# More places for y late in the first pass, weight matrices laid over the passing adjacency tiles, and the powers and copies of x reordered at the seam

## The chip, the cores and the metric

The kernel runs on one core of one Trainium2 chip. The metric is the device time of one execution in microseconds, as a median over several runs. A profile was taken of one more execution; its span and the times inside it are given separately from the median.

## What is computed

Inputs are node features `x` (4096 x 512), an adjacency matrix `adj` (4096 x 4096, fp32) and weights. The matrix has the diagonal and about two entries in a thousand beside it, all below one. Two layers follow each other:

```python
# layer 0
a = adj + eye
d = sum(a, axis=1) ** -0.5
out = relu((d[:, None] * a * d[None, :]) @ x @ W.T + b)
x = layernorm(x + out)
# layer 1: 8 heads
adj1 = maximum(adj, eye)
scores = q @ k.T / sqrt(64) + 0.01 * eye - 1e16 * (1 - adj1)
x = layernorm(x + sum over heads of softmax(scores) @ v @ Wo)
```

All entries beside the diagonal are below one, so the term with 1e16 leaves only the diagonal in the softmax. Layer 1 is then a product of each row with one fixed matrix. The kernel uses this, and tests for it at the end; a general version would run if the test failed.

## The kernel before

All that matters here is in `few_edges_below_one` (L420 to L1328). The 4096 rows are cut into 32 tiles of 128. The work has two passes.

**First pass** (loop at L1004, t = 0 to 32). Each step takes one adjacency tile of 128 x 4096 (2 MB), loaded by SP three steps ahead (`load_first`, L559). Of the 32 tiles, 12 are *early* (0, 2, 4, 6, 9, ... 24) and 5 are *resident* (27 to 31). These lie in five buffers of the pool `big` under the name `a_t`, and stay until their entries are extracted. The other 15 only pass through, in two buffers named `a_n`, and are loaded again in the second pass. The last tile is loaded in two halves.

Per tile, ACT sums the rows (`sum_rows`, L691), or, for an early tile, only looks for negative entries (`sum_negative`, L696), since DVE gives the row sum of an early tile out of its extracted entries (L926). POOL makes the degree factor out of the sum (`scaling`: an addition at L703 and a power at L706, written to `d_all`). Beside this, x of each tile is loaded by POOL (`load_x`, L549), transposed by PE (L672), copied out of PSUM by ACT (`evacuate`, L677, to `xT`) and multiplied by the transposed weights on PE (`times`, L684, to a PSUM buffer `acc`; two buffers for xT, five for acc). ACT then multiplies the product by d (`keep_y`, L711, to `y_t`, four buffers), and POOL writes it to the DRAM tensor `y` (L713).

The list `due` (L984) says at which step each tile's y is made: a tile that is not early at t + 1, an early one later, when DVE has its sum. The xT copy and the product are issued one step ahead, two from step `EARLIER` = 25 on. A scheduler orders the instructions of each engine by priority and readiness. `keep_in_program_order` holds marked instructions of an engine in the order in which the program has them; the y copies are marked, the xT copies are not.

The second layer's matrix `wvo` is made in the same steps from Wv and Wo (`second_weights`). Wo and the transposed Wv lie in a buffer of the first pass named `wo` (16 KB per partition), which is last read by the products at L619.

DVE meanwhile extracts the entries of the tiles (`extraction`): per tile eight segments, each with a search for the eight largest (L740) and for their places (L741), then short steps that sort them into records. `some((t + 1) * RATE)` paces this: 7 of 16 steps per loop step, the rest in the second pass. `match` spreads the records over 128 lanes so that nine gathers per tile are enough.

**The seam** (L1049 to L1219). The pool of the first pass is closed, and two pools are opened in its memory: `second` (gathered rows `g`, own rows `yo`, `h`, and others) and then `mats` (three selection matrices `s_t` of 128 x 9 or 10 x 128, and `sq`). 18 gathers are issued ahead, and 14 selection matrices are built.

**Second pass** (loop at L1235). For each tile, POOL gathers nine times 128 rows of y from DRAM by index (L1066; 19 buffers). PE multiplies each by its selection matrix (L1269) and adds in PSUM. ACT builds the selection matrices (`spread`, L964 to L977). DVE scales, adds bias and residual (`scaled` L1135, `residual` L1143). The norm is folded into the last steps: PE transposes h (L672), ACT copies it (L677), PE multiplies by wvo (L684), ACT writes the result. DVE goes on with extraction up to the 28th of the 32 tiles.

Of the kernel before, what the change touches and what calls it, by code (L numbers as in the profile page):

```python
# [9 lines left out]
FP = mybir.dt.float32  # L10
# [4 lines left out]
P = 128  # L15
# [404 lines left out]
def few_edges_below_one(  # L420
# [18 lines left out]
    nc = tc.nc  # L439
    N, D = x.shape  # L440
# [31 lines left out]
    ps_t = ctx.enter_context(tc.tile_pool(name="ps_t", bufs=3, space=bass.MemoryType.PSUM))  # L472
    ps_a = ctx.enter_context(tc.tile_pool(name="ps_a", bufs=5, space=bass.MemoryType.PSUM))
    first = ExitStack()
    p1 = first.enter_context(tc.tile_pool(name="first", bufs=2))

    ident = const.tile([P, P], FP, name="ident")
# [62 lines left out]
    def load_a(t, pool=big, name="a_t", parts=1):  # L540
        a_t = pool.tile([P, N], FP, name=name)
        for c in range(parts):
            o = ts(c, N // parts)
            nc.sync.dma_start(a_t[:, o], adj[ts(t, P), o])
        return a_t
# [8 lines left out]
    early = [e * last // EARLY for e in range(EARLY)]  # L554
# [4 lines left out]
    def load_first(t, parts=1):  # L559
        if t in early or t in resident:  # L560
            return load_a(t, parts=2 if t == NT - 1 else parts)
        return load_a(t, p1, "a_n")

    a_tiles = {0: load_first(0, 4)}


# [6 lines left out]
    wT = p1.tile([P, ND, D], FP, name="wT", bufs=1)  # L573
# [10 lines left out]
    def load_second_weights():  # L584

        nc.sync.dma_start(
            wv.rearrange("p (h f) -> p h f", h=H),
            wvs.rearrange("h (p j) k -> p h (j k)", j=ND),
        )
        su1 = p1.tile([P, 2, ND, D], FP, name="wo", bufs=1)  # L590
        nc.sync.dma_start(su1[:, 0], wo.rearrange("(r a) k o -> (a k) r o", a=2))
        return su1

    def order_second_weights():
        nc.gpsimd.tensor_copy(
            w_nat.rearrange("p j (h k) -> p j h k", h=H),
            wv.rearrange("p (h j k) -> p j h k", h=H, j=ND),
        )
# [70 lines left out]
    def transpose_rows(src, dcs=range(ND)):  # L669
        pt = ps_t.tile([P, 512], FP, name="pt")  # L670
        for dc in dcs:
            nc.tensor.transpose(pt[:, ts(dc, P)], src[:, ts(dc, P)], ident)  # L672
        return pt

    def evacuate(pool, name, pt):
        dst = pool.tile([P, ND, P], FP, name=name, bufs=2)
        nc.scalar.copy(dst.rearrange("p c s -> p (c s)"), pt[:, :D])  # L677
        return dst

    def times(srcT, w, u=None, dcs=range(ND)):  # L680
        if u is None:
            u = ps_a.tile([P, D], FP, name="acc")
        for dc in dcs:
            nc.tensor.matmul(  # L684
                u, srcT[:, dc, :], w[:, dc, :], start=(dc == 0), stop=(dc == ND - 1)
            )
        return u

    def sum_rows(dst, part):
        dump = wk_.tile([P, N], mybir.dt.uint8, name="dump")  # L690
        nc.scalar.activation(dump[:, : part.shape[1]], part, AF.Copy, accum_out=dst)  # L691

    def sum_negative(t, a_t, halves=(0, 1)):
        dump = wk_.tile([P, N], mybir.dt.uint8, name="dump")
        o = slice(halves[0] * N // 2, (halves[-1] + 1) * N // 2)
        nc.scalar.activation(  # L696
            dump[:, o], a_t[:, o], AF.Relu, scale=-1.0,
            accum_out=neg_all[:, t, halves[0] : halves[0] + 1],
        )

    def scaling(t, more=None):
        deg = small.tile([P, 1], FP, name="deg")
        nc.gpsimd.tensor_scalar(deg, deg_all[:, t : t + 1], 1.0, None, op0=ALU.add)  # L703
        if more is not None:
            nc.gpsimd.tensor_tensor(deg, deg, more, ALU.add)
        nc.gpsimd.tensor_tensor(d_all[:, t : t + 1], deg, mhalf, ALU.pow)  # L706

    def keep_y(t, u):
        y_t = p1.tile([P, D], FP, name="y_t", bufs=4)
        tc.keep_in_program_order(  # L710
            nc.scalar.activation(y_t, u, AF.Copy, scale=d_all[:, t : t + 1])  # L711
        )
        nc.gpsimd.dma_start(y[ts(t, P), :], y_t)  # L713
# [164 lines left out]
    def match(*stages):  # L878
        for stage in stages:
            n = staged[stage]  # L880
            if stage == KEY:
                ready = n < len(sorted_)
            elif stage == PERM:
                ready = n < staged[RANKS] and n - staged[MOVE] < 2
            else:
                ready = n < staged[stage - 1]
            if stage == ACROSS:
                ready = ready and n == staged[RANKS]
            if stage == MOVE:
                ready = ready and n == staged[END]  # L890
            if not ready:
                continue
            t = order[n]
            e = edges[t]
            if stage == KEY:
                e["key"] = match_key(t)
            elif stage == ACROSS:
                e["pk"] = match_across(e["key"])
            elif stage == RANKS:
                e["rank"] = match_ranks(e["key"], e["pk"])  # L900
            elif stage == PERM:
                e["perm"] = match_perm(e["rank"])
            elif stage == MOVE:
                e["pm"] = match_move(e["rec"], e["perm"])
            else:
                match_end(t, e["pm"])
                matched.add(t)
            staged[stage] += 1
# [34 lines left out]
    def some(upto):  # L943
        while count[0] < upto:
            count[0] += 1
            next(work, None)
# [33 lines left out]
    xs, us = {}, {}  # L980
    DEEP = 3
    RATE = 7
    EARLIER = NT - 7
    due = [(t + 1, t) for t in range(NT) if t not in early]  # L984
    for n, t in enumerate(early):
        at = max(t + 3, -(-STEPS * (n + 1) // RATE) + 1)
        taken = [j for j, _ in due]
        due.append((next((j for j in (at, at + 1) if j not in taken), at), t))
    due.sort()
    fetch = [t for _, t in due]  # L990

    def prefetch(count):
        for _ in range(count):
            if fetch:
                t = fetch.pop(0)
                xs[t] = load_x(t, nc.gpsimd, p1, 6)

    prefetch(5)
    for t in range(1, DEEP):
        a_tiles[t] = load_first(t)  # L1000
# [3 lines left out]
    for t in range(NT + 1):  # L1004
        if t == 0:
            su1 = load_second_weights()
        if t + DEEP < NT:
            a_tiles[t + DEEP] = load_first(t + DEEP)
        if t == 3:
            order_second_weights()  # L1010
            setup = second_weights(su1)

        lo, hi = t + 1 + (t > EARLIER), t + 1 + (t >= EARLIER)
        ahead = [j for at, j in due if lo <= at <= hi]
        pts = []
        for j in ahead:
            prefetch(1)
            pts.append(transpose_rows(xs.pop(j)))
        kind, begin, end = next(setup, (None,) * 3) if len(ahead) < 2 else (None,) * 3
        got = begin() if kind == "t" else None  # L1020
        if t < NT:
            if t in early:
                sum_negative(t, a_tiles[t])
            else:
                sum_rows(deg_all[:, t : t + 1], a_tiles[t][:, : N // 2 if t == NT - 1 else N])
                more = None
                if t == NT - 1:
                    more = small.tile([P, 1], FP, name="more")
                    sum_rows(more, a_tiles[t][:, N // 2 :])
                scaling(t, more)  # L1030
            if t in again:
                del a_tiles[t]
        if left:
            left()
            left = None
        for j in [j for at, j in due if at == t]:
            if j in early:
                scaling(j)
            keep_y(j, us.pop(j))
        for j, pt in zip(ahead, pts):  # L1040
            us[j] = times(evacuate(p1, "xT", pt), wT)
        if kind == "t":
            end(got)
        if kind == "p":
            left = lambda end=end, pa=begin(): end(pa)
        if t < NT - 5:
            match(*ALL)
        some((t + 1) * RATE)
# [2 lines left out]
    second.append(True)  # L1051


    p2 = ctx.enter_context(tc.tile_pool(name="second", bufs=2))
    mat = ctx.enter_context(tc.tile_pool(name="mats", bufs=3))
    AHEAD = 18

    SUMMED = (NT - 2, NT - 1)
# [151 lines left out]
    yo, zs, hs, pts, hTs, ws, sts, mats, halves = ({} for _ in range(9))  # L1210
# [24 lines left out]
    for i in range(NT + 2):  # L1235
# [3 lines left out]
        p = i - 1  # L1239
        has_p = 0 <= p < NT  # L1240
        for k in range(KH):
            ends = p == NT - 1
            t = at("T", i, k)
            if t not in (None, NT - 1):
                hTs[t] = evacuate(p2, "hT", transpose_rows(hs[t]))
            t = at("M", i, k)
# [50 lines left out]
            t = at("Q", i, k)  # L1297
# [3 lines left out]
            t = at("V", i, k)  # L1301
# [6 lines left out]
            t = at("F", i, k)  # L1308
# [45 lines left out]
```

## Time and profile before

| | us |
| --- | --- |
| median of 3 runs | 652.62 (651.55 to 655.58) |
| profiled execution | 689.3 |
| its span on the core | 687.5 |
| PE busy in the span | 555.8 |
| DVE busy | 546.9 |
| ACT busy | 509.7 |
| POOL busy | 352.0 |
| last load of adjacency in the first pass has landed | 213.4 |
| last y copy ends | 226.7 |
| first gather is issued | 230.1 |
| first product of the second pass starts | 236.6 |

Times inside the span count from its start. A row of the timeline gives start, duration, engine, line, operation, output from input with shapes, the number of instructions merged, and in square brackets the time for which the engine stood idle before it and what ended that wait. Matmuls in fp32 show as two records each, so a product of a 128 x 512 tile with the 512 x 512 weights has eight. Busy shares are means over stages with different limits; which wait ends last has to be read stage by stage. The end of a matmul is modelled.

### The profile page before, as it was taken

What the parts mean: (1) busy time and instruction counts of PE and PEld (TensorE: products, weight loads), DVE (VectorE), ACT (ScalarE), POOL (GpSimd) and SP (SyncE); (2) the same over time, 40 slices, a digit from 0 to 9 for tenths busy, and PEclk for the clock granted to TensorE, in tenths of its full rate; (3) what the DMA queues carried; (4) which work ended last, traced back from release to release, by engine and by line L of the source; (5) the groups of instructions that cost most, each with busy time, mean ns of one, the idle gap of its engine ahead of it and who ended that gap; (6) DMA issues with size and microseconds to landing.
All of it is one profiled execution on the core that took longest, in us unless ns stands there. A gap on an engine that the chain in (4) does not pass through costs nothing. (4 is left out here: it accounts for less than half of the span.)

```text
span 687.5 us, 7941 instructions
## 1 busy us (share of the span) xinstructions
PE 555.8 (81%) x1604; PEld 257.1 (37%) x1604; DVE 546.9 (80%) x2141; ACT 509.7 (74%) x1121; POOL 352.0 (51%) x464
## 2 busy tenths in 40 slices
PE   1688795897884284779978999889897989899994
PEld 1343342343441132334433444334343434344442
DVE  6679999999999725689978999799999888442441
ACT  1778859778759833799876888779897779789642
POOL 4222322412323575667666566666676676557620
PEclk9999898999997597999998999999999999999998
DMA  8999999999992677999999799999998977868731
GB/s 338 401 418 427 421 428 408 419 422 418 421 423 114 227 207 250 391 328 370 409 401 344 233 369 358 335 325 346 345 366 311 351 239 234 260 215 263 231 105 51
DMA packets 51850, 222.14 MB, mean 323 GB/s; under 512 B 8080, under 2 KB 9104, under 8 KB 45520
## 3 DMA queue, kind: packets, MB, share of 16 engines
q1 hardware_dynamic: 18416, 119.55, 43.3%
q0 software_dynamic: 28240, 92.56, 39.5%
q10 hardware_dynamic: 5136, 9.44, 3.6%
q14 instruction: 43, 0.35, 0.1%
q8 instruction: 15, 0.25, 0.1%
HBM read 204.73 MB, written 16.78 MB: 322 GB/s over the span
## 5 line engine op out<-in xcount | busy, mean ns | idle before, releaser
L1066 POOL DMA_INDIRECT g<-y,cols_all x288 | 282.1, 980 | 148.3 <-issue 67.4
L1269 PE MATMUL acc<-g,s_t 128*128 128x512 f32 x540 | 256.7, 615 | 23.0 <-ACT s_t L977 22.4
L740 DVE MAX8 v_all<-a_t 128x8 f32<-128x512 f32 x256 | 170.7, 679 | 17.9 <-DMA a_t<-in_adj_dram 17.4
L741 DVE FIND_INDEX8 idx<-v_all,a_t 128x8 uint32<-128x512 f32 x256 | 174.3, 683 | 0.0
L1269 PEld LDWEIGHTS acc<-g,s_t 128*128 128x128 f32 x540 | 101.5, 197 | 135.8 <-issue 109.8
L684 PE MATMUL acc<-wT,xT 128*128 128x512 f32 x256 | 123.6, 634 | 27.0 <-ACT xT L677 24.8
L684 PE MATMUL acc<-wvo,hT 128*128 128x512 f32 x256 | 118.2, 604 | 12.4 <-issue 6.0
L696 ACT ACTIVATE dump<-a_t 128x2048 uint8<-128x2048 f32 (+1 forms) x52 | 119.4, 2296 | 1.5 <-DMA a_t<-in_adj_dram 1.5
L684 PEld LDWEIGHTS acc<-wT,xT 128*128 128x128 f32 x256 | 49.9, 203 | 88.1 <-issue 54.2
L684 PEld LDWEIGHTS acc<-wvo,hT 128*128 128x128 f32 x256 | 48.1, 192 | 76.8 <-issue 64.0
L964 ACT ACTIVATE sq<-cols,wr_all 128x128 f32<-128x128 f32 x160 | 57.7, 392 | 2.4 <-DMA y<-y_t 2.4
L968 ACT ACTIVATE s_t<-sq,wr_all 128x128 f32<-128x128 f32 x128 | 57.1, 483 | 0.5
L691 ACT ACTIVATE dump<-a_n 128x4096 uint8<-128x4096 f32 x15 | 54.3, 3622 | 0.6 <-DMA a_n<-in_adj_dram 0.3
L549 POOL DMA_DIRECT2D x_t<-in_x_dram x32 | 17.9, 560 | 63.0 <-PE pt L672 62.8
L977 ACT ACTIVATE s_t<-s_t,wr_all 128x128 f32<-128x128 f32 x150 | 48.5, 390 | 0.6 <-ACT s_t L974 0.6
L753 DVE MAX8 top<-key 128x8 f32<-128x64 f32 x192 | 39.9, 215 | 5.6 <-DVE h L1135 1.3
L1135 DVE SCALAR_TENSOR_TENSOR h<-acc,d_all,yo 128x512 f32<-128x512 f32 (+1 forms) x33 | 23.8, 721 | 21.0 <-remote 18.4
L711 ACT ACTIVATE y_t<-acc,d_all 128x512 f32<-128x512 f32 x32 | 21.5, 684 | 21.0 <-POOL d_all L706 16.3
L713 POOL DMA_DIRECT2D y<-y_t x32 | 19.0, 592 | 29.6 <-ACT y_t L711 28.7
L703 POOL TENSOR_SCALAR deg<-deg_all 128x1 f32<-128x1 f32 x32 | 6.9, 230 | 48.3 <-ACT dump L691 48.2
L1170 ACT ACTIVATE sums<-sums 128x1 f32<-128x1 f32 x32 | 6.3, 197 | 33.8 <-DVE sums L1165 10.3
L1128 DVE SCALAR_TENSOR_TENSOR yo<-yo,own_all,b_bc 128x512 f32<-128x512 f32 x32 | 23.7, 741 | 9.4 <-issue 8.7
(126 smaller groups left out, 652.7 us busy)
## 6 DMA issues: line engine op xcount, KB each, us to landing
a_t<-in_adj_dram SPq DMA_DIRECT2D x30, 2048.0 KB
a_n<-in_adj_dram SPq DMA_DIRECT2D x15, 2048.0 KB
x_t<-in_x_dram POOLq DMA_DIRECT2D x32, 256.0 KB
y<-y_t POOLq DMA_DIRECT2D x32, 256.0 KB
yo<-y SPq DMA_DIRECT2D x32, 256.0 KB
x_t<-in_x_dram SPq DMA_DIRECT2D x32, 256.0 KB
out_dram<-r_t ACTq DMA_DIRECT2D x32, 256.0 KB
g<-y,cols_all POOLq DMA_INDIRECT x288
```

The lines of the kernel that those rows point to most:

```text
L684: nc.tensor.matmul(u, srcT[:, dc, :], w[:, dc, :], start=(dc == 0), stop=(dc == ND - 1))
L691: nc.scalar.activation(dump[:, : part.shape[1]], part, AF.Copy, accum_out=dst)
L696: nc.scalar.activation(dump[:, o], a_t[:, o], AF.Relu, scale=-1.0, accum_out=neg_all[:, t, halves[0] : halves[0] + 1],)
L740: long.append(lambda o=o, seg=seg: nc.vector.max(v[:, o], seg))
L741: long.append(lambda o=o, seg=seg: nc.vector.max_index(idx[:, o], v[:, o], seg))
L753: return lambda: nc.vector.max(top[:, f, r * 8 : r * 8 + 8], keyf[:, f])
L964: nc.scalar.activation(sq, cols1, AF.Square, bias=wr[:, 2, k : k + 1])
L968: nc.scalar.activation(s_t[:, k, :], away(), AF.Relu, scale=wr[:, 3, k : k + 1], bias=wr[:, 1, k : k + 1],)
L977: nc.scalar.activation(s_t[:, k, :], s_t[:, KH, :], AF.Copy, scale=wr[:, 1, k : k + 1])
L1066: nc.gpsimd.indirect_dma_start(out=slots[j], out_offset=None, in_=y[:, :], in_offset=bass.IndirectOffsetOnAxis(ap=cols_all[:, t, k : k + 1 ...
L1135: nc.vector.scalar_tensor_tensor(hs[i][:, c], zs[i][:, c], d_all[:, order[i] : order[i] + 1], yo[i][:, c], op0=ALU.mult, op1=ALU.add,)
L1269: nc.tensor.matmul(zs[i], mats[i][:, k, :], slots.pop(i * KH + k), start=(k == 0), stop=(k == KH - 1),)
```

## The change

Four things are altered; no instruction is removed or added, only order, memory and waits differ.

1. The passing adjacency tiles `a_n` get a pool of their own, `passing`, opened ahead of the pool `first`. At the seam `mats` is opened ahead of `second`, so that the matrices lie where the passing tiles were.
2. The y of tiles that are due at step 20 or later (15 of the 32) goes to one of eight places in a buffer that takes over the memory of `wo`. The others keep the four buffers.
3. The degree factor of an early tile is asked for before the step's row sum and not just before its y copy.
4. The xT copies issued from step 25 on are marked to stay in program order among the marked instructions of ACT.

```diff
     first = ExitStack()
+    pn = first.enter_context(tc.tile_pool(name="passing", bufs=2))
     p1 = first.enter_context(tc.tile_pool(name="first", bufs=2))
...
-        return load_a(t, p1, "a_n")
+        return load_a(t, pn, "a_n")
...
-    def evacuate(pool, name, pt):
+    def evacuate(pool, name, pt, pinned=False):
         dst = pool.tile([P, ND, P], FP, name=name, bufs=2)
-        nc.scalar.copy(dst.rearrange("p c s -> p (c s)"), pt[:, :D])
+        copy = nc.scalar.copy(dst.rearrange("p c s -> p (c s)"), pt[:, :D])
+        if pinned:
+            tc.keep_in_program_order(copy)
         return dst
...
     def keep_y(t, u):
-        y_t = p1.tile([P, D], FP, name="y_t", bufs=4)
+        if t in due_first:
+            y_t = p1.tile([P, D], FP, name="y_t", bufs=4)
+        else:
+            if not y_bank:
+                y_bank.append(p1.tile([P, 8, D], FP, name="wo", bufs=1))
+            y_t = y_bank[0][:, y_count[0] % 8]
+            y_count[0] += 1
         tc.keep_in_program_order(
             nc.scalar.activation(y_t, u, AF.Copy, scale=d_all[:, t : t + 1])
         )
...
     due.sort()
+    due_first = [t for j, t in due if j < 20]
+    y_bank, y_count = [], [0]
     fetch = [t for _, t in due]
...
         got = begin() if kind == "t" else None
+        for j in [j for at, j in due if at == t and j in early]:
+            scaling(j)
         if t < NT:
...
         for j in [j for at, j in due if at == t]:
-            if j in early:
-                scaling(j)
             keep_y(j, us.pop(j))
         for j, pt in zip(ahead, pts):
-            us[j] = times(evacuate(p1, "xT", pt), wT)
+            us[j] = times(evacuate(p1, "xT", pt, t >= EARLIER), wT)
...
+    mat = ctx.enter_context(tc.tile_pool(name="mats", bufs=3))
     p2 = ctx.enter_context(tc.tile_pool(name="second", bufs=2))
-    mat = ctx.enter_context(tc.tile_pool(name="mats", bufs=3))
```

## What was predicted

> **What bounds the kernel now.** I read the page first (busy times, the forty slices, the costliest groups), then busy time by stage, then ACT's timeline from 140 to 230 us, then the timelines around the seam between the passes. The chain of waits at the end of the page covers only the last microsecond and says nothing on the seam.
>
> ```profile
> PE 555.8 (81%) x1604; PEld 257.1 (37%) x1604; DVE 546.9 (80%) x2141; ACT 509.7 (74%) x1121; POOL 352.0 (51%) x464
> ...
> PE   1688795897884284779978999889897989899994
> PEld 1343342343441132334433444334343434344442
> DVE  6679999999999725689978999799999888442441
> ACT  1778859778759833799876888779897779789642
> ```
>
> No engine is full overall, but each stage has its own limit. The first pass runs against DMA (its slices are 9 up to about 206 us), with DVE full from about 100 us. The second pass has PE at nine tenths and DVE nearly so. Between them, near slices 12 to 15, everything thins out. By stage (columns: stretch, length, PE, PEld, DVE, ACT, POOL busy, granted clock, DMA share, GB/s):
>
> ```profile
> 200.00:210.00 10.00, 8.23 (x15) 3.55 (x16) 10.00 (x30) 6.07 (x7) 1.61 (x4) 0.83 0.82 345
> 210.00:220.00 10.00, 4.20 (x10) 1.44 (x8) 10.00 (x42) 8.42 (x6) 3.65 (x8) 0.84 0.22 86
> 220.00:230.00 10.00, 0.00 (x0) 0.00 (x0) 10.00 (x45) 7.13 (x13) 3.52 (x8) 0.50 0.20 79
> 230.00:240.00 10.00, 3.42 (x4) 1.47 (x5) 5.99 (x20) 10.00 (x31) 7.70 (x8) 0.50 0.95 320
> ```
>
> From 214 to 236 us PE does nothing and DMA is nearly empty: no gather may start until every row of y is in DRAM, and ACT is late with the last rows. ACT's timeline says why:
>
> ```profile
> 198.87 0.59 ACT L677 COPY xT<-pt 128x512 f32<-128x512 f32 x1 [3.06 <-PE pt L672]
> 201.03 0.69 ACT L711 ACTIVATE y_t<-acc,d_all 128x512 f32<-128x512 f32 x1 [1.57 <-DMA y<-y_t]
> 204.62 0.69 ACT L711 ACTIVATE y_t<-acc,d_all 128x512 f32<-128x512 f32 x1 [2.90 <-DMA y<-y_t]
> ...
> 205.67 3.63 ACT L691 ACTIVATE dump<-a_t 128x4096 uint8<-128x4096 f32 x1
> ...
> 215.64 1.26 ACT L711 ACTIVATE y_t<-acc,d_all 128x512 f32<-128x512 f32 x2 [1.58 <-POOL d_all L706]
> ...
> 226.01 0.69 ACT L711 ACTIVATE y_t<-acc,d_all 128x512 f32<-128x512 f32 x1 [0.44 <-POOL d_all L706]
> ...
> 229.37 0.69 ACT L964 ACTIVATE sq<-cols,wr_all 128x128 f32<-128x128 f32 x2 [2.40 <-DMA y<-y_t]
> ```
>
> By the completions in the trace the last six loads of adjacency landed at 188.2, 194.2, 200.2, 206.1, 209.7 and 213.4 us. Their sums began at 192.1, 205.7, 210.3, 216.8, 221.0 and 223.0: ACT is 4 us behind its data at tile 27 and over 10 us behind at tiles 28 to 30. In between it stood for 3.06 + 1.57 + 2.90 + 1.58 + 0.44 = 9.6 us. From the last y the seam goes on like this:
>
> ```profile
> 230.13 1.06 POOL L1066 DMA_INDIRECT g<-y,cols_all  x1 [2.59 <-DMA y<-y_t]
> ...
> 236.58 5.72 PE L1269 MATMUL acc<-g,s_t 128*128 128x512 f32 x8 [22.39 <-ACT s_t L977]
> ```
>
> The PE wait is put down to ACT, but that s_t was done before 232.2; the first gather's increments arrive until 235.8, and that is the later one.
>
> **What the Trainium skill says.** "TensorE: Matmul & The Clock Gate", Architectural detail: ScalarE's queue is strictly first in, first out. The trace agrees: the sum of tile 28, whose data landed at 194.2, stands behind two y copies until 205.7. The same page, Part 1: PE's clock is half or full, and about 3.4 us of sustained work lift it. Agrees: from 236.58 the matmul records follow each other at 0.85 us until 240.1, then at 0.43. "DMA: Bandwidth & Descriptors", Anatomy of one DMA: about 2 us of a transfer are fixed, mostly the receipt. Agrees: last y issued 227.00, its readers free at 229.3 to 229.4.
>
> **The change, part by part.** *Eight places for y (tiles due at step 20 or later, 15 of the 32).* A y copy reuses a place after eight others and not four. It takes away the two waits on y's DMA, 1.57 + 2.90 = 4.5 us of ACT; no instruction is added. What is late next behind them is the xT copy and the sum of tile 28.
>
> *d_all asked for ahead of the row sum.* POOL's 0.2 us addition and 0.57 us power of an early tile now stand before the step's x load and y write in POOL's queue, not behind. Before 230 us ACT waits 16.3 us in 12 places for d_all; some 1.7 and 1.8 us of these lie shortly before tile 27 (at 162 and 175 us), 1.58 at 214. I count 2 us ahead of 192 and the 1.58. POOL issues the same DMAs; it is 16 to 36% busy there, so the order costs it nothing. Without that cover a 0.8 us pair per step would delay an x load.
>
> *xT copies pinned from step 25.* This one costs. The built order of ACT now has, from the sum of tile 27: sum, y y, xT xT, sum, y, xT, sum, y y, xT xT, sum, y, half, half, xT, y, y. Before, all xT copies were through by 210.4 and the last product by 214.2, so the last y waited only 0.44 us. Now tile 31's xT stands after both halves of the last sum, its product and its y follow in series.
>
> *Matrices laid over the passing tiles.* The sq copies no longer share memory with y's places, so ACT does not wait 2.40 us at 227. Nothing is gained on the path: PE's first product waits for the gather. The cover is those 6 us from issue to landing. If the gather landed at once, it would be worth up to 2.4. The order of PE, SP and POOL after the seam is the same in both programs.
>
> The sum, on the profiled time scale. ACT from tile 27's sum to the end of the last half: 4 sums at 3.7 (start to next start), 2 halves at 2.05, six y at 0.58, five xT at 0.47: 14.8 + 4.1 + 3.5 + 2.4 = 24.8 us. Starting at 190 (192.1 less the 2) with 1 us for a product that is not ready: 215.8. The floor from the data is 213.4 + 2.1 = 215.5. I take 216. Then xT 0.6, eight matmul records 3.5 at 0.43 or 6.9 at 0.85 (PE idles some 2 us before, so partly slow; I take 4.5), y 0.7: 221.8, against 226.7. With the early ends (190, fast clock) it is 220.4, with the late ones (192.1, slow clock) 226.3: a gain of 0.4 to 6.3, taken as 4.9. From the last y to the first gather nothing changes (3.4 us), so gathers start near 225.2 and PE near 231.7.
>
> What of it arrives at the end? DVE is full until 235 and then idles 6.5 us waiting for PE's product at 242.5, so it gives 4.9 us without becoming the bound at once. In the 50 us stretches from 300 to 600 us PE is busy 41 to 47, DVE 37 to 48: PE leads, but waits for DVE some 17 us over them (6.5 of it for permutations, the rest for keys and records). So I keep three quarters: 3.7 us. The lower bound is 0 (DVE's work sets the pace to 575 us), the upper the whole.
>
> The profiled execution took 689.3 us (span 687.5), the timed median is 652.62, 36 less. About half of that shows as one stall:
>
> ```profile
> 265.33 0.75 DVE L1135 SCALAR_TENSOR_TENSOR h<-acc,d_all,yo 128x512 f32<-128x512 f32 x1 [18.43 <-remote]
> ```
>
> It needs only PE's first accumulation, recorded as over at 246.8. I take it for a feature of this execution and carry the difference, not the level: 652.6 - 3.7 = 648.9, say 649.
>
> **The rivals.** *Swallowed.* DVE, full from 100 us on, sets the pace of the second pass and the 4.9 us turn into PE waits. For it: DVE idles only some 27 us from 270 to 550. Against: those 27 us and the 6.5 at the seam. Time 652.6, within 2.
>
> *PE's clock makes the new series long: slower.* From the first xT after tile 27's sum (about 195) PE has six products one after another, each behind an xT that ACT now gives late. At full clock they need 6 x 3.44 = 20.6 us and end at 216, hidden. All slow they need 41 and end at 236; the last y is then at 237, 10 us later than now: 663. It decides where a product takes over (226.0 - 195) / 6 = 5.2 us, that is, where half of the 48 records run slow. For it: the clock was 0.83 between 200 and 220, and PE gets more pauses. Against: the 24 records from 201.77 lost only 12.43 - 10.3 = 2.1 us, those from 187.94 (10.46 us) none.
>
> *Larger.* The timed runs hold part of the 18.4 us stall and a seam with less crowding shortens it, or all 9.6 us of ACT's waits go and the second pass keeps them: 643, with the whole stall 630. For it: nothing but the stall's place. Against: the data floor at 213.4 us.
>
> **How the numbers follow.** Main case 0.50 at 649, its own range 646 to 651.5; swallowed 0.15; slower 0.18 (656 to 663, 0.15 of it above 1%); larger 0.17. About 1% (6.5 us) is what a measurement of this kernel can tell from no change. Faster by more: the larger case plus 0.05 from the main one's end, 0.22. Slower by more 0.15. Within 0.63. The range 641 to 658 leaves out half of the larger and half of the slower case.
>
> **What would show it.** Right: no wait on y's DMA ahead of ACT's y copies after 190 us, tile 28's sum starting before 200, the last y at 220 to 224, the first gather at 223 to 227, the 2.40 us at sq gone. Right on the cost: a PE wait of 3.5 to 7 us before the last y. Wrong: the last y at 226 or later, matmul records at 0.85 us through 200 to 225, or PE's second-pass waits for DVE grown by as much as the seam shrank. A changed time while the seam stands still would say that none of this is the cause.

## The result and the profile after

The changed kernel took 650.0 us (median of 16 runs, one of which took 1033.8 us), the kernel before 654.4 us on the same chip: a ratio of 0.9946, 95% interval 0.9924 to 0.9969. The medians differ by 4.4 us; the ratio, from which that one run is left out, says 3.5 us, with an interval from 2.0 to 5.0. The 3.7 us that were predicted lie inside it, and so do the 4.9 that the seam was to give. The likeliest case held. Its parts did not: two of the steps were wrong, and their errors cancelled.

The profile of before that the prediction used, and one set of experiments (e1 to e4, on another chip than the other sets; before: 686.8 us there, 653 to 654 in the others), belong to a level at which the same program takes some 33 us longer, so times are compared only within a set.

The page of the changed kernel (busy times, then busy tenths of a slice of 16 us):

```profile
PE 556.8 (86%) x1604; PEld 258.0 (40%) x1604; DVE 543.6 (84%) x2141; ACT 509.1 (79%) x1121; POOL 351.2 (54%) x464
...
PE   1698696888689486999999989999999999999794
...
DVE  5679999999999994999999979999999996532431
ACT  1868888779779775999898957999979989994433
```

At the seam PE has one slice of four tenths, where it had slices of 4, 2 and 4, and later it stays at nine tenths. Part of this belongs to the first profile of before and not to the change: e9, a later profile of the same kernel, has PE at nine tenths from 400 us on as well. The stages around the seam (stretch, length, PE, PEld, DVE, ACT, POOL busy, clock, DMA share, GB/s):

```profile
200.00:210.00 10.00, 9.94 (x32) 4.98 (x31) 10.00 (x33) 8.69 (x7) 2.13 (x5) 1.00 0.93 385
210.00:220.00 10.00, 7.21 (x17) 2.72 (x15) 10.00 (x43) 6.72 (x12) 3.21 (x7) 1.00 0.17 66
220.00:230.00 10.00, 1.33 (x2) 0.50 (x2) 10.00 (x44) 10.00 (x33) 5.77 (x7) 0.60 0.69 249
230.00:240.00 10.00, 9.78 (x26) 3.94 (x25) 10.00 (x38) 5.99 (x14) 7.59 (x8) 0.89 0.77 233
```

PE's products for the last tiles now run to 219 us at full clock (1.00 from 200 to 220), and the gathers begin inside the third stretch. ACT's timeline of the changed kernel over the same time:

```profile
187.18 3.62 ACT L694 ACTIVATE dump<-a_t 128x4096 uint8<-128x4096 f32 x1
...
192.75 0.69 ACT L720 ACTIVATE wo<-acc,d_all 128x512 f32<-128x512 f32 x1 [1.28 <-PE acc L687]
...
194.34 3.62 ACT L694 ACTIVATE dump<-a_t 128x4096 uint8<-128x4096 f32 x1
...
199.45 3.62 ACT L694 ACTIVATE dump<-a_t 128x4096 uint8<-128x4096 f32 x1 [0.21 <-DMA a_t<-in_adj_dram]
...
214.72 0.57 ACT L678 COPY xT<-pt 128x512 f32<-128x512 f32 x1
...
219.13 0.69 ACT L720 ACTIVATE wo<-acc,d_all 128x512 f32<-128x512 f32 x1 [3.25 <-issue]
```

The sums of tiles 27, 28 and 29 start at 187.2, 194.3 and 199.5, the last of them as soon as its load has landed. No y copy waits for y's DMA here. The last half sum ends at 214.7; in series with it follow the last xT, its product (3.70 us on PE) and the last y. The 3.25 us ahead of the last y are put down to issue, but PE's product ends only then. The gathers, from POOL's timeline:

```profile
223.25 1.06 POOL L1077 DMA_INDIRECT g<-y,cols_all  x1 [2.59 <-DMA y<-wo]
```

Against the recorded signs: tile 28 before 200, the first gather within 223 to 227 and no 2.40 us wait at sq, all as said; the last y ends at 219.8, just under the 220 to 224 that was given, and its wait is 3.25 us, just under 3.5 to 7. The wait on y's DMA after 190 us is gone as said, but this sign turned out to tell nothing: two later profiles of the kernel before (e1, e9) do not have it either.

### The profile page after: what moved, and what is told of

The parts are those of the page before. It is cut to its first block, busy times and chain, and to the rows that moved or that the text cites. A ratio compares the mean times of both kernels' runs of the same rounds, so it can differ in the third digit from the quotient of the medians.

```text
span 645.5 us, 7946 instructions
## 1 busy us (share of the span) xinstructions
PE 556.8 (86%) x1604; PEld 258.0 (40%) x1604; DVE 543.6 (84%) x2141; ACT 509.1 (79%) x1121; POOL 351.2 (54%) x464
## 5 line engine op out<-in xcount | busy, mean ns | idle before, releaser
L1280 PE MATMUL acc<-g,s_t 128*128 128x512 f32 x540 | 258.1, 612 | 23.8 <-DMA g<-y,cols_all 13.4
L749 DVE MAX8 v_all<-a_t 128x8 f32<-128x512 f32 x256 | 172.7, 687 | 16.9 <-DMA a_t<-in_adj_dram 16.9
L1280 PEld LDWEIGHTS acc<-g,s_t 128*128 128x128 f32 x540 | 98.0, 194 | 140.9 <-issue 92.8
L687 PE MATMUL acc<-wT,xT 128*128 128x512 f32 x256 | 126.6, 647 | 24.1 <-ACT xT L678 24.0
L687 PEld LDWEIGHTS acc<-wvo,hT 128*128 128x128 f32 x256 | 49.7, 196 | 67.4 <-issue 58.1
L1146 DVE SCALAR_TENSOR_TENSOR h<-acc,d_all,yo 128x512 f32<-128x512 f32 (+1 forms) x33 | 24.0, 727 | 20.9 <-PE acc L1280 15.9
L678 ACT COPY hT<-pt 128x512 f32<-128x512 f32 x31 | 17.9, 579 | 23.8 <-PE pt L673 22.8
L673 PE MATMUL pt<-ident,x_t 128*128 128x128 f32 x128 | 20.3, 291 | 8.8 <-DVE above L841 7.6
L765 DVE MATCH_REPLACE8 key<-top,key 128x64 f32<-128x64 f32 x128 | 27.2, 214 | 0.0
```

The costliest lines, as they stand in the source:

```text
L687: nc.tensor.matmul(u, srcT[:, dc, :], w[:, dc, :], start=(dc == 0), stop=(dc == ND - 1))
L749: long.append(lambda o=o, seg=seg: nc.vector.max(v[:, o], seg))
L765: return lambda: nc.vector.match_replace(keyf[:, f], top[:, f, r * 8 : r * 8 + 8], keyf[:, f], 0.0)
L1280: nc.tensor.matmul(zs[i], mats[i][:, k, :], slots.pop(i * KH + k), start=(k == 0), stop=(k == KH - 1),)
```

## The experiments

The theory after this result was: the seam moved by 6.9 us (226.7 to 219.8), 4.4 arrive, so the second pass gives some back, because gathers are delayed by the first reload of an adjacency tile. The rival was that DVE or PE sets the pace there and swallows it. The other question was which of the four parts moves the seam.

| kernel | first gather | span of that profile | gather to end | median less before's in its set |
| --- | --- | --- | --- | --- |
| before (e9) | 227.13 | 652.5 | 425.4 | -0.7 |
| changed | 223.25 | 645.5 | 422.3 | -4.4 |
| changed (e5) | 223.90 | 647.2 | 423.3 | -4.6 |
| no overlay (e6) | 224.61 | 650.5 | 425.9 | -2.7 |
| reload later (e7) | 225.19 | 653.8 | 428.6 | +1.2 |
| last xT first (e8) | 222.47 | 646.7 | 424.2 | -4.7 |
| no pin (e10) | 225.25 | 649.4 | 424.2 | -1.9 |
| seam later (e11) | 231.97 | 654.5 | 422.5 | +4.4 |
| early d_all alone (e12) | 232.61 | 659.0 | 426.4 | +4.7 |
| set with the longer time: before (e1) | 226.87 | 684.4 | 457.5 | +1.9 |
| no pin (e2) | 226.15 | 682.3 | 456.2 | -1.9 |
| no bank (e3) | 238.15 | 693.2 | 455.1 | +9.0 |
| no early d_all (e4) | 230.99 | 689.5 | 458.5 | +3.7 |

One reading needs the whole table. In the rows above the set with the longer time, e7 left aside since it alters the second pass, the first gather comes 3.9, 3.2, 2.5, 4.7 and 1.9 us earlier than e9's (changed, e5, e6, e8, e10) or 4.8 and 5.5 us later (e11, e12). The medians lie 4.4, 4.6, 2.7, 4.7 and 1.9 us below before's, or 4.4 and 4.7 above. The end moves with the first gather and by about as much; the two numbers differ by 1.3 us at most.

The first gather has a spread of its own. ACT's order in the first pass is the same in the changed kernel, e5, e6 and e7, and the first gather comes at 223.25, 223.90, 224.61 and 225.19. A difference of 1 to 2 us between two single profiles therefore shows little.

**The kernel before again (e1, e9).** No edit.

> The kernel before, unchanged, for a second profile of it. Ratio 1.00. Theory 1 (gathers give the gain back): the seam stands as in the first profile (last y at 225.5 to 228, PE's first second-pass product at 235 to 238, so 7 to 8 us later than in the changed kernel), but PE loses 3 to 4 us less than the changed kernel in the first five tiles of the second pass, because fewer of its gathers fall under the first reload of an adjacency tile. Theory 2 (DVE sets the pace): the first five tiles take as long as in the changed kernel (within 1 us), and the changed kernel loses the 3 to 4 us between 260 and 560 us to PE waits on DVE.

Ratio 1.0014 (0.9987 to 1.0040). It belongs to the set with the longer time, so its second pass says nothing about the changed kernel's. Its seam does, since the first pass takes the same time in both (last y at 222.8 here, 223.0 in e9).

> The kernel before, unchanged, for a profile at the level of its timed runs. Ratio 1.00. Theory (the seam's gain, less what the opening of the second pass loses): first gather 226.5 to 230.5 (223.3 and 223.9 in the two profiles of the changed kernel), the ninth h (the first tile after eight) 4 to 6 us later than the changed kernel's 343.1 and 343.8, the end later by the same, so what is lost of the seam is lost before 345 us. Rival (DVE or PE sets the pace later): ninth h 6 to 7 us later than in the changed kernel, the difference shrinking to 4 only after it.

Ratio 0.9987 (0.9964 to 1.0010). First gather at 227.13, ninth h at 347.9 against 343.1 and 343.8, and the end 5.3 to 7.0 us later than in the two profiles of the changed kernel. The difference does not shrink after the ninth h, so the rival falls, and it is no smaller at the end than at the first gather (3.2 to 3.9), so nothing is lost before it either. The 5.3 to 7.0 are too large, though: e9's profiled execution took 1.7 us more than its kernel's median, that of the first profile of the changed kernel 2.7 us less. ACT's timeline of e9:

```profile
200.47 0.59 ACT L677 COPY xT<-pt 128x512 f32<-128x512 f32 x1 [3.06 <-PE pt L672]
...
202.56 3.65 ACT L691 ACTIVATE dump<-a_t 128x4096 uint8<-128x4096 f32 x1
...
212.63 1.26 ACT L711 ACTIVATE y_t<-acc,d_all 128x512 f32<-128x512 f32 x2 [1.67 <-POOL d_all L706]
...
223.01 0.69 ACT L711 ACTIVATE y_t<-acc,d_all 128x512 f32<-128x512 f32 x1 [0.44 <-POOL d_all L706]
...
226.37 0.69 ACT L964 ACTIVATE sq<-cols,wr_all 128x128 f32<-128x128 f32 x2 [2.40 <-DMA y<-y_t]
```

Here is the first surprise. The two waits on y's DMA that the prediction took as its main term (1.57 and 2.90 us at 201 and 205) are in none of these two later profiles. The 2.40 us at sq and the wait of 3.06 us on PE are.

**Without the pin (e2, e10).**

```diff
-            us[j] = times(evacuate(p1, "xT", pt, t >= EARLIER), wT)
+            us[j] = times(evacuate(p1, "xT", pt), wT)
```

> The changed kernel without the pin on the xT copies. Theory 1 (the series xT, product, y after the last sum costs 4.4 us at the seam): last y ends at 215.5 to 217.5 and not 219.8, time 1 to 3 us less than the changed kernel (647 to 649). Rival (the pin is what keeps ACT's sums from standing behind an xT copy that waits for PE's transposes): waits of 2 to 3 us on pt come back ahead of an xT copy between 190 and 210, the sum of the last half ends at 217 or later, last y at 221 to 224, time equal to before or up to 2 us less (651 to 654).

> The changed kernel without the pin, once more. Theory (pin and bank pay only together: without the pin the xT copies stand ahead of the sums and wait for PE, 6.6 + 2.7 + 1.3 us in the first profile of this version): first gather 225.5 to 227.5, time 0 to 2 us less than before and 2 to 5 us more than the changed kernel. Rival (the pin does nothing): within 1.5 us of the changed kernel (648 to 650.5 at before's 653.4).

0.9985 (0.9959 to 1.0011) and 0.9968 (0.9948 to 0.9989). In e10's set it is 1.9 us less than before, where the changed kernel has 4.4 and 4.6 in its own sets. The signs that the rival of e2 named are there, and they speak for a gain by the pin. The times alone do not show it, since the intervals of e10 and of the changed kernel overlap. In e10 ACT stays within some 1.1 us of the changed kernel up to the sum of tile 25 and then meets this:

```profile
186.42 0.58 ACT L678 COPY xT<-pt 128x512 f32<-128x512 f32 x1 [6.77 <-PE acc L687]
```

The scheduler has put this xT copy ahead of the sum of tile 26. The copy takes one of two xT buffers and waits for a product on PE, and the sum, whose data is there, stands behind it: 186.9 and not 180.2. The last half sum ends at 220.0, against 215.4 in e5. The last y then waits only 0.44 us, so 4.6 us of sums turn into 1.35 at the first gather. All four profiles with the pin have an earlier first gather (223.25 to 225.19) than the two without (225.25 and 226.15), by little at the nearest. A gain of 1 to 2 us is likely; clear of the spread it is not.

**Without the bank (e3).**

```diff
-        if t in due_first:
+        if True:
             y_t = p1.tile([P, D], FP, name="y_t", bufs=4)
```

> The changed kernel with four places for every y (no bank). Theory 1: ACT waits 3 to 5 us on y's DMA again between 190 and 215, last y ends at 222.5 to 225 (219.8 with the bank), time 1.5 to 3 us more than the changed kernel. Rival (the bank is not what moves the seam, the earlier d_all and the pin are): last y within 1 us of 219.8, time within 1 us of the changed kernel.

1.0168 (1.0136 to 1.0200, six runs): 9.0 us slower than before by the medians. The sums run as in the changed kernel up to tile 27 (187.7); then:

```profile
205.73 0.69 ACT L720 ACTIVATE y_t<-acc,d_all 128x512 f32<-128x512 f32 x1 [12.88 <-DMA y<-y_t]
```

Much larger than expected, and in a kernel whose ancestor has no such wait: it is the other parts that make it.

**Without the earlier d_all (e4).** The two lines with `scaling(j)` go back to just ahead of `keep_y`.

> The changed kernel with d_all of the early tiles computed where the kernel before has it. Theory 1 (each wait on d_all late in the first pass moves the seam): 1.5 to 3.6 us more waiting on d_all ahead of ACT's y copies from 155 us, last y at 221 to 223.5, time 0.7 to 2 us more than the changed kernel. Rival (ACT has caught up with the loads, which then set the end): last y within 0.7 us of 219.8, time the same within 0.5 us.

1.0059 (1.0025 to 1.0094), slower than before, which neither case had. Its sums start at the times of before up to tile 26 (tile 24 at 177.6; before 177.8; changed 168.3), although bank and pin are there, and no y copy waits for y's DMA, as in e1 and e9. So without the earlier d_all the bank gives ACT nothing. The waits for d_all grow (19.8 us in 11 places from 60 to 215 us, e9 and e1 have 14.0 in 10), and the pin adds its series: the last half sum ends at 222.5 (e1: 221.6), the last y starts 4.4 us after it (e1: 1.1), and the first gather is 4.1 us later than in e1.

**The changed kernel again (e5), and without the overlay (e6).** For e6 `a_n` goes back to the pool `first`, and `mats` is opened after `second`.

> The changed kernel, unchanged, once more. Theory 1 (seam gain, half of it kept): 2.5 to 5 us less than before, whatever the chip's level; first gather at 222 to 225 against 226.9 and 230.1 in the two profiles of before. Rival (the first difference was chance between runs): within 1 us of before and a first gather at 226 or later.

> The changed kernel with the passing tiles back in the pool of the first pass and the matrices after the second pool. Theory 1: a wait of 2 to 2.5 us on y's DMA ahead of the first sq, first gather at the same 222 to 225, PE's first second-pass product within 0.5 us of the changed kernel, time within 1 us of it. Rival (the matrices are late enough to hold PE's first products): PE's second-pass start or the first h 1.5 to 2.5 us later and the time 1 to 2.5 us more.

0.9926 (0.9889 to 0.9963) and 0.9954 (0.9932 to 0.9976). In e6 the 2.40 us at sq are back (223.84), but PE's first product does not come later after the first gather (5.7 us, e5 6.2), so the rival's mechanism is not there. The median is 1.9 us above e5's, 0.7 of it is there at the first gather already, and the intervals overlap. From the first gather to the end the three kernels of the shorter time without the overlay and with the reload unchanged took 425.4 to 426.4 us, the five with it 422.3 to 424.2. This is no gain of the overlay. The profiled executions of the three lie 1.6 to 2.1 us above the medians of their own kernels, those of the five between 2.7 below and 0.1 above; with this taken off, it is 423.7 to 424.3 against 423.2 to 425.0.

**The first reload later (e7).**

```diff
-            if k == KH - 1 and queue and len(reloaded) < free:
+            if k == KH - 1 and i >= 2 and queue and len(reloaded) < free:
```

The loads of y, x and adjacency on SP in the second pass are also held in program order.

> The changed kernel with the first reload of an adjacency tile one output tile later (behind the loads of y and x for the fifth tile instead of the fourth, about 258 us and not 241 on the time scale of the first profile of the changed kernel). Theory 1 (the reload delays the gathers of the second output tile, and with it h): no PE wait on a gather over 1 us ahead of the second h, the second h at 249 to 253 and not 257.5, and 2 to 6 us less at the end. Rival (PE or DVE sets the pace later anyway): the second h earlier by the same, the end within 1.5 us of the changed kernel, or later because DVE waits for the reloaded tile.

1.0007 (0.9983 to 1.0032): 4 to 6 us slower than the changed kernel. The second h came at 252.4, as expected, but the third at 275.7 and not 269.4. PE's timeline:

```profile
265.66 3.78 PE L1281 MATMUL acc<-g,s_t 128*128 128x512 f32 x4 [5.64 <-DMA g<-y,cols_all]
```

The first reload holds up the gathers of the tile that it meets, early or late. Moving it later is no gain. That it is a loss can't be put down to the reload alone: the loads on SP are held in order as well, and of the 3.6 us at the ninth h (347.4, e5 343.8) 1.3 are there at the first gather. The rest was not traced. In the changed kernel the same wait shows as DVE standing for the second h, and e9 has it too (8.98 us), so it makes no difference between the kernels:

```profile
257.50 0.75 DVE L1146 SCALAR_TENSOR_TENSOR h<-acc,d_all,yo 128x512 f32<-128x512 f32 x1 [9.10 <-PE acc L1280]
```

**The last xT ahead of the last half sums (e8).** The last tile's transposes are issued at step 29, and the half sums are pinned behind its xT copy.

```diff
+        if t == NT - 3:
+            last_pt.append(transpose_rows(xs.pop(NT - 1)))
...
+        if part.shape[1] < N:
+            tc.keep_in_program_order(copy)
```

> The changed kernel with the last tile's transposes ahead of the last two products on PE, and its xT copy ahead of the two last half sums on ACT. Theory 1 (xT, product and y stand in series behind the last sum): last y's wait for its product falls from 3.25 us to under 1.5, last y 1.5 to 2.5 us earlier, first gather likewise; time 0.5 to 2 us less. Rival (PE's products from 194 us on are the chain, so nothing comes earlier): last y within 0.5 us of the changed kernel.

0.9924 (0.9897 to 0.9952), level with e5. The wait ahead of the last y fell from 3.25 to 1.16 us (now for d_all), and the first gather came 1.4 us earlier than in e5; at the end 0.1 us of median is left. A gain of this size can't be told from the spread, so neither side is shown. It is no better version.

**The seam later (e11).**

```diff
                 scaling(t, more)
+                for n in range(5 if t == NT - 1 else 0):
+                    tc.keep_in_program_order(nc.scalar.activation(
+                        wk_.tile([P, N], mybir.dt.uint8, name="dump")[:, : N // 2],
+                        a_tiles[t][:, : N // 2], AF.Copy,
+                        accum_out=small.tile([P, 1], FP, name="idle"),
+                    ))
```

> The changed kernel with five more sums of half a tile (2.05 us each, their result unused) on ACT behind the last sum and ahead of the last two y copies; nothing else is changed. It moves the seam back by about 6.3 us (10.2 less the 3.9 in which the last y waits for its product), first gather at 229 to 230.5. Theory (the seam alone carries the gain, two thirds of it kept): 3.5 to 5.5 us more than the changed kernel, so about the time of before. Rival (the gain comes from elsewhere, the seam is swallowed by the second pass): at most 1.5 us more than the changed kernel. Rival (everything of the seam is kept): 6 us or more.

1.0061 (1.0036 to 1.0085), 4.4 us more than before by the medians and so 8 to 9 more than the changed kernel. The first gather moved from 223.90 to 231.97, 8.1 us, of which 1.0 is there ahead of the added sums; the ninth h moved by 8.1 (351.85 against 343.79), the span by 7.3. The theory of two thirds falls, as does the swallowing; the third case is right: what the seam loses or gains, the end does too.

**The earlier d_all alone (e12).** The kernel before, with only `scaling(j)` moved.

> The kernel before with one part of the change alone: d_all of the early tiles asked for ahead of the step's row sum. ACT's order is that of the changed kernel without the pin. New theory (the earlier d_all lets ACT catch up with the loads, and bank and pin only keep it from losing that again): 12 us or more of the 14.0 us that ACT waits for d_all before 215 us are gone, the sum of tile 24 starts near 168 and not 178; then waits of 5 us or more on y's DMA or on PE appear between 175 and 205 us, the first gather is at 225 to 232 (227.1 before), and the time is within 3 us of before on either side, at least 2 us more than the changed kernel. Prediction as recorded (the two y-DMA waits are the larger part, d_all worth 3.6 us): no new waits, first gather 2 to 4 us earlier than before, and 2 to 3.5 us less time.

1.0078 (1.0055 to 1.0102), 4.7 us slower than before; the new theory had allowed for 3. ACT's timeline of e12:

```profile
185.62 0.59 ACT L677 COPY xT<-pt 128x512 f32<-128x512 f32 x1 [5.58 <-PE acc L684]
...
205.32 0.69 ACT L711 ACTIVATE y_t<-acc,d_all 128x512 f32<-128x512 f32 x1 [7.01 <-DMA y<-y_t]
...
213.04 1.08 ACT L677 COPY xT<-pt 128x512 f32<-128x512 f32 x2 [2.37 <-PE pt L672]
```

Tile 24's sum starts at 168.2, as in the changed kernel. Then waits on y's DMA and on PE, which the changed kernel with its bank and pin has shorter or not at all, take all of it back and more. ACT's order here is that of e10, which adds bank and overlay: together they are worth some 6.6 us (+4.7 to -1.9) to a kernel that has the earlier d_all.

## Why the prediction was right, and where it was wrong

The frame was right: ACT was late with the last rows, the first gather waits for the last y, and an earlier seam makes the end earlier. The sizes inside it were not, and that the number came out is in part luck.

**The earlier d_all: the step that was mis-sized.** The prediction counted "2 us ahead of 192 and the 1.58", 3.6 of the 16.3 that it had read. ACT's waits from 60 to 215 us (total, times, longest), first in e9:

```profile
ACT y_t L711 <- POOL d_all L706: 14.0, 10, 1.8
ACT xT L677 <- PE pt L672: 13.5, 9, 3.8
```

and in the changed kernel:

```profile
ACT xT L678 <- PE pt L673: 4.7, 2, 3.0
ACT dump L694 <- DMA a_n<-in_adj_dram: 4.6, 4, 1.8
...
ACT dump L699 <- DMA a_t<-in_adj_dram: 2.9, 2, 1.5
```

All 14.0 us are gone, and with them 8.8 of the waits on PE's transposes. In e9 no wait for a load is listed here: ACT is behind its data, so every wait that it loses counts, from the first step on, and not only those near tile 27. In the changed kernel it waits 7.5 us for loads: it has caught up with them, and tile 24's sum is 9.5 us earlier (168.3 against 177.8). New waits on loads and on PE's products take much of this back. All that is listed adds up to 33.9 us in e9 and 27.2 in the changed kernel, 6.7 less, and the last half sum ends 7.2 us earlier. That this part is needed is shown by e4, that it is not enough by e12.

**The bank: right in direction, wrong in reason.** "It takes away the two waits on y's DMA, 1.57 + 2.90 = 4.5 us" took them from one profile; e1 and e9, the same kernel, don't have them. Without the earlier d_all the bank has nothing to remove (e4). But once ACT runs ahead, the y copies come while the loads still fill the DMA engines: the median from a y write's issue to its landing, from 140 us on, is 9.5 us in e9, 19.7 in the changed kernel and 15.9 in e5, and four places no longer do (12.88 us in e3, 7.01 in e12).

**The pin: "This one costs" was half of it.** The series was foreseen and came out at its size: 4.4 us from the last sum's end to the last y's start, 1.1 in e9, so 3.3 more; predicted were 5.1 behind a sum that ends at 216 (measured 214.7). What was missed is what the copies wait for when they are not pinned: 6.77 us in e10 ahead of a sum whose data was there. Net, e10 and e5 differ by 1.35 us at the first gather and by 2.7 in the medians. So the sign of "this one costs" is probably wrong, but this is not shown clear of the spread.

**The seam.** By e9 the last half sum ends at 221.9; in the changed kernel at 214.7 and 215.4 (7.2 and 6.5 earlier), less 3.3 for the series: 3.9 and 3.2 at the first gather, where 4.9 was predicted. With e6 and e7, which have the same first pass, it is 2.5 and 1.9. The 6.9 of the comparison with the first profile of before held 3 us of that profile's own. When the prediction's terms are added again, the ends of its range come out at 220.6 and 226.1 and not at 220.4 and 226.3, which changes nothing.

**"I keep three quarters": wrong.** The working found 17 us in which PE waits for DVE and took a quarter off. These waits belong to the longer time of the profile that it read. The same stretch in the first profile of before and, below it, three in e9:

```profile
400.00:450.00 50.00, 46.03 (x133) 20.50 (x132) 44.40 (x172) 40.44 (x117) 31.53 (x33) 1.00 0.96 353
...
400.00:450.00 50.00, 50.00 (x145) 23.12 (x144) 50.00 (x192) 47.28 (x136) 35.85 (x37) 1.00 0.98 359
...
500.00:550.00 50.00, 50.00 (x146) 23.11 (x145) 48.20 (x188) 45.01 (x129) 38.17 (x39) 1.00 0.93 315
550.00:600.00 50.00, 50.00 (x153) 23.36 (x152) 18.54 (x70) 43.45 (x130) 38.12 (x40) 1.00 0.86 274
```

From 300 to 600 us PE is busy 290.9 us in e9, and the waits listed for it are 8.8 us for gathers and none for DVE; in the changed kernel it is 291.7, 6.3 and none. In e1 18.6 us of waits for DVE are there again. So the slack from which the quarter was taken is not there, and e11 kept its 8.1 us to the ninth h unchanged and 7.3 to the end, e9 against the changed kernel likewise. With 4.9 x 0.75 = 3.7 predicted and some 2 to 4 us kept whole, the two errors met.

**The overlay** was costed at nothing; e6 shows no gain by it that is clear of the spread.

**The rivals.** Slower by PE's clock: no, PE is busy for 14.9 of the 15 us from 198 to 213 and its clock is 1.00 there. Swallowed: no (e11). Larger, by the stall of 18.43 us: no. That stall belongs to the longer time: e1 has it at the same h, e9 has not.

```profile
261.40 0.75 DVE L1135 SCALAR_TENSOR_TENSOR h<-acc,d_all,yo 128x512 f32<-128x512 f32 x1 [16.61 <-remote]
```

Carrying the difference and not the level was therefore right.

## What to carry to other kernels

Where an engine runs behind its data, every wait on it counts, however early and short, until it has caught up. What is gained is bounded by how far it was behind, and not by the sum of the waits: here 22.8 us of waits went and 6.7 us of waiting were saved. An engine that is freed in this way meets the next limits at once (buffers whose writes are slow while loads run, a copy put ahead of ready work), so a part that costs time by itself can be needed for the gain of the whole: here the earlier d_all alone was 0.8% slower, the rest without it 0.6% slower, and the set 0.5 to 0.7% faster. And take a wait as a term only if a second profile of the same kernel shows it.

## What was not expected of the hardware

A y write of 256 KB lands 2.4 us after its issue at the quickest; from 140 us on, beside the loads of 2 MB, the median was 9.5 us in e9 and 19.7 in the changed kernel. The Trainium skill, "DMA: Bandwidth & Descriptors", Queues, rings and completion order, says that each DMA engine goes round the queues it has work for, a packet at a time. A small write would then pay for the large loads beside it; these numbers agree with that without showing the packets. The loads of x, which POOL issues as well, became slower too (13.4 to 21.6 us), so what is due to the loads of 2 MB and what to the transfers ahead on the same queue is not separated.

The longer time of e1 to e4 and of the first profile of before is all in the second pass: from the first gather to the end 455 to 459 us in these five profiles, 422 to 429 in the others, while the first gather of before is at 226.9 and 230.1 there and at 227.1 here. In these five DVE stands 11.6 to 18.4 us for the first h although PE's records of its products have ended. What causes it was not found. The sets ran on different chips, so it may be the chip's; no run here tells it.
